# An attention loop that takes two steps per turn, in a fused two-layer graph network

## Chip, cores and metric

The kernel runs on one core of one Trainium2 chip. The metric is the device time of one execution in microseconds; runs of a kernel are taken beside runs of the kernel before on the same chip. All runs told here are of the same (fast) state: a kernel's executions agree within 0.25%.

## The reference, cut to what matters

Layer 0 (a graph convolution with batch norm) ends with `out = batchnorm(h @ W2.T)`; its last normalization is left to the second layer's loop. The changed loop computes layer 1 for 16 batches of 1024 nodes with 256 features, all in float32:

```python
x  = layernorm(x + layer0(x))                        # x1 in the kernel
c  = mean over features of x                         # cs, crow
A  = |(|sigmoid(c[m] - c[n]) - 0.5|) - 0.5| * 2      # per batch, 1024 x 1024
Wg = adj * A                                         # wg
q  = relu((x^T @ Wg) * para)                         # pg -> qT, 4 heads of 64
k, v = split(x @ kv_w)                               # pk -> kT, pv -> v
out = softmax(q k^T * scale) v                       # s -> e -> o, denominators pd
x  = layernorm(x + out)                              # pf, r
```

## The kernel before

Names that the profile uses: `s` scores (TensorE), `e` their exponentials (ScalarE), `acc` sums of e (VectorE), `o` values. One **step** handles two heads, 512 queries and 256 keys; 16 steps make a batch, which I call a **window**. Beside the attention of batch b, a schedule `at` prepares batches b+1 (keys, values, graph matmuls) and b+2 (load, batch norm, layer norm, transposes, graph weights).

```python
        ps_s = pool("ps_s", 2, space=PSUM)   # scores: 2 tiles of two banks
        ps_o = pool("ps_o", 1, space=PSUM)
        ps_t = pool("ps_t", 3, space=PSUM)   # shared by py, px, pc, pk, pv, pg, pd, pf
        # ... (cut)
        def bn2(b, j):                       # VectorE: batch norm of layer 0 (yt)
            for c in range(CT):
                t = yts[b, j][:, c, :]
                nc.vector.tensor_scalar(t, t, s2[:, c : c + 1], t2[:, c : c + 1], op0=OP.mult, op1=OP.add)
        # ...
        def ln1_a(b, j):                     # TensorE py, then VectorE
            p = ps_t.tile([P, FB], F32, tag="t", name="py")
            for c in range(CT):
                nc.tensor.transpose(p[:, ts(c, P)], yts[b, j][:, c, :], ident)
            # ... x1 = p + x, statistics
        def x1_t(b, j):                      # TensorE px, then ScalarE
            p = ps_t.tile([P, FB], F32, tag="t", name="px")
            for c in range(CT):
                nc.tensor.transpose(p[:, ts(c, P)], x1s[b, j][:, ts(c, P)], ident)
            nc.scalar.copy(x1Ts[b][:, :, ts(j, P)], p[:, :C].rearrange("p (c n) -> p c n", c=CT))
        # ...
        def wg_b(b, i):                      # VectorE, behind two ScalarE passes of wg_a
            t = wgs[b, i]
            nc.vector.scalar_tensor_tensor(t, t, 1.0, adj_sb[:, i, :], op0=OP.add, op1=OP.mult)
        # ... (cut: crow (pc), keys (pk), values (pv), graph (pg), scores (s), attend (o),
        #      dens (pd), finish_a (pf), finish_b)
        def put(w, s, f, *a):
            at.setdefault(w * NS + s, []).append((f, a))

        for b in range(B):
            put(b - 2, 4, begin, b)
            for j in range(NT):
                put(b - 2, 3 + j, load, b, j)
                put(b - 2, 4 + j, bn2, b, j)
                put(b - 2, 5 + j, ln1_a, b, j)
                put(b - 2, 6 + j, ln1_b, b, j)
                put(b - 2, 7 + j, x1_t, b, j)
            put(b - 2, 7 + NT, crow, b)
            for i in range(NT):
                put(b - 2, 8 + NT + i, wg_a, b, i)
                put(b - 2, 8 + NT + i, wg_b, b, i)
            # ... (cut: keys, values, graph of b - 1; dens and finish of b)

        for g in range(min(at), max(last, nsteps - 1) + 1):
            if 0 <= g + 1 < nsteps:
                scores(g + 1)
                exps(g + 1)
            if 0 <= g < nsteps:
                sums(g)
            for f, a in at.get(g, []):
                f(*a)
            if g == load_weights_at:
                load_weights()
            if 0 <= g < nsteps:
                attend(g)
```

Of the kernel before, what the change touches and what calls it, by code (L numbers as in the profile page):

```python
# [22 lines left out]
def gnn_norm_attention_kernel(  # L23
# [276 lines left out]
    def load_weights():  # L300
        nc.sync.dma_start(kvw, kv_w.rearrange("(c p) f -> p c f", p=P))
        for i in range(0, NT, 2):
            nc.sync.dma_start(
                adj_sb[:, i : i + 2, :], adj[i * P : (i + 2) * P, :].rearrange("(c p) m -> p c m", p=P)
            )
        nc.sync.dma_start(para_sb, para.rearrange("o (c p) h w -> p c (o h w)", p=P))
# [14 lines left out]
    def fast():  # L321
      with ExitStack() as fx:
        pool = lambda name, bufs, **k: fx.enter_context(tc.tile_pool(name=name, bufs=bufs, **k))
        ldp = pool("ldp", 3)
        x1p = pool("x1p", 21)
        x1Tp = pool("x1Tp", 1)
        crp = pool("crp", 1)
        wgp = pool("wgp", NT)
        kp = pool("kp", 2 * CT)
        qp = pool("qp", CT + 1)  # L330
        vp = pool("vp", 2)
        ep = pool("ep", 5)
        accp = pool("accp", 3)
        otp = pool("otp", 3)
        sm = pool("sm", 4)
        rp = pool("rp", 4)
        ps_s = pool("ps_s", 2, space=PSUM)
        ps_o = pool("ps_o", 1, space=PSUM)
        ps_t = pool("ps_t", 3, space=PSUM)
# [104 lines left out]
        def step(g):  # L444
            b, s = divmod(g, NS)
            hf, pair, cp = s // (NP * NT // 2), s // (NT // 2) % NP, s % (NT // 2)
            return b, hf, pair, cp

        def scores(g):
            b, hf, pair, cp = step(g)  # L450
            for a in range(2):
                cb = 2 * cp + a
                t = ps_s.tile([P, 2, FB], F32, tag="s", name=f"s{g}_{a}")
                for h in range(2):
                    nc.tensor.matmul(  # L455
                        t[:, h, :],
                        kTs[b, pair][h * HD : (h + 1) * HD, ts(cb, P)],
                        qTs[b, pair][h * HD : (h + 1) * HD, ts(hf, FB)],
                        start=True,
                        stop=True,  # L460
                    )
                S[g, a] = t

        def exps(g):
            for a in range(2):
                E[g, a] = ep.tile([P, 2, FB], F32, tag="e", name=f"e{g}_{a}")
                nc.scalar.activation(E[g, a], S.pop((g, a)), AF.Exp)  # L467

        def sums(g):
            b, hf, pair, cp = step(g)  # L470
            if cp == 0:
                ACC[b, hf, pair] = accp.tile([P, 2, FB], F32, tag="acc", name=f"acc{g}")
                nc.vector.tensor_add(ACC[b, hf, pair], E[g, 0], E[g, 1])
            else:
                for a in range(2):
                    nc.vector.tensor_add(ACC[b, hf, pair], ACC[b, hf, pair], E[g, a])  # L476

        def attend(g):
            b, hf, pair, cp = step(g)
            if cp == 0:  # L480
                O[b, hf, pair] = ps_o.tile([P, FB], F32, tag="o", name=f"o{g}")
            for a in range(2):
                cb = 2 * cp + a
                for h in range(2):
                    nc.tensor.matmul(  # L485
                        O[b, hf, pair][h * HD : (h + 1) * HD, :],
                        vs[b][:, cb, pair * P + h * HD : pair * P + (h + 1) * HD],
                        E[g, a][:, h, :],
                        start=(cb == 0),
                        stop=(cb == NT - 1),  # L490
                    )
                E.pop((g, a))
            if cp == NT // 2 - 1:
                t = otp.tile([P, FB], F32, tag=f"ot{pair}", bufs=2 - pair, name=f"ot{g}")
                nc.scalar.copy(t, O.pop((b, hf, pair)))
                OT[b, hf, pair] = t
# [38 lines left out]
        at = {}  # L535
# [32 lines left out]
                put(b, s + 1 + i % (FB // P), finish_a, b, i)  # L568
                put(b, s + 2 + i % (FB // P), finish_b, b, i)

        last = max(at)
        nsteps = B * NS
        load_weights_at = -2 * NS + 3
        for g in range(min(at), max(last, nsteps - 1) + 1):
            if 0 <= g + 1 < nsteps:
                scores(g + 1)
                exps(g + 1)
            if 0 <= g < nsteps:
                sums(g)
            for f, a in at.get(g, []):  # L580
                f(*a)
            if g == load_weights_at:
                load_weights()
            if 0 <= g < nsteps:
                attend(g)

    fast()


# [169 lines left out]
```

## Time and profile before

| | kernel before |
|---|---|
| time, median of four runs | 2861.15 us (2859.72 to 2862.74) |
| span of the profiled run | 2855.9 us |
| one window, 16 steps | 115.08 us |
| idle of TensorE in a window | 1.32 us, before the pc transposes |

The window is the distance between the starts of the first s burst of one batch and of the next. Only windows 0 to 13 prepare a batch two ahead; window 14 prepares only one ahead, window 15 none. The prediction below shows the lines that carry the reading: TensorE is the bound, so look for time between matmul starts and for its waits.

### The profile page before, as it was taken

The numbers are of one execution on the slowest core, as the hardware profiler recorded it, in microseconds if no ns is written. First come the engines' busy times: TensorE is split into PE (matmuls) and PEld (weight loads), VectorE is DVE, ScalarE is ACT, GpSimd is POOL, SyncE is SP. The second block draws the span as 40 slices with busy tenths as digits, with TensorE's granted clock in tenths as the row PEclk, the third lists the DMA queues.
The fourth block names the chain that finished last, engine by engine and source line by source line (L and its number), as shares of the span: only waits on it lengthen the run. The fifth ranks groups of instructions, "written<-read, shape, count | busy, mean of one in ns | idle before, by whom it ended". The sixth has DMA issues, their size and how long they took to land.

```text
span 2855.9 us, 25725 instructions
## 1 busy us (share of the span) xinstructions
PE 2751.3 (96%) x9426; PEld 1170.7 (41%) x9426; DVE 1502.2 (53%) x2717; ACT 1162.0 (41%) x1487; POOL 377.5 (13%) x523
## 2 busy tenths in 40 slices
PE   7999999999899599999999999999999999999997
PEld 5444444444344244434434344344343443434332
DVE  3011111012444457667686686776766857668556
ACT  1111111112741155645546455364464553644633
POOL 0000000000000112122121221221212212113012
PEclk7999999999999699999999999999999999999998
DMA  3121122120463410001010010010100100101000
GB/s 104 59 88 59 74 88 78 70 103 0 158 232 111 151 30 25 28 19 39 19 32 30 16 43 24 23 35 18 38 30 15 41 20 29 34 13 43 8 10 22
DMA packets 109988, 146.97 MB, mean 51 GB/s; under 512 B 10272, under 2 KB 92704, under 8 KB 103712
## 3 DMA queue, kind: packets, MB, share of 16 engines
q1 hardware_dynamic: 109856, 145.27, 14.9%
q8 instruction: 76, 1.25, 0.2%
q14 instruction: 56, 0.46, 0.1%
HBM read 86.52 MB, written 58.72 MB: 51 GB/s over the span
## 4 chain that ended last, share of the span: by engine, by line
PE 96%; DVE 2%; DMA 1%; POOL 0%; ACT 0%; issue 0%; SPq 0%; POOLq 0%; ACTq 0%
PE s L455 17%; PE o L485 17%; PE pg L435 16%; PE pa L201 15%; PE po L264 8%; PE ph L214 8%; PE pk L408 4%; PE pv L419 4%; PE pf L515 2%; PE pd L504 1%; PE py L364 1%; PE px L377 1%; PE pd L172 1%; PE pc L388 1%; PE pf L516 0%; DMA yt<-yT 0%
## 5 line engine op out<-in xcount | busy, mean ns | idle before, releaser
L467 ACT ACTIVATE e<-s 128x1024 f32<-128x1024 f32 x512 | 496.5, 1022 | 480.7 <-PE s L455 479.4
L455 PE MATMUL s<-qT,kT 64*128 64x512 f32 x2048 | 508.7, 615 | 0.0
L485 PE MATMUL o<-e,v 128*64 128x512 f32 x2048 | 495.7, 605 | 0.0
L476 DVE TENSOR_TENSOR acc<-acc,e 128x1024 f32<-128x1024 f32 x384 | 468.7, 1221 | 41.7 <-ACT e L467 27.8
L435 PE MATMUL pg<-wg,x 128*128 128x512 f32 x1024 | 477.2, 604 | 0.2 <-ACT x1T L378 0.2
L201 PE MATMUL pa<-AhT,x 128*128 128x512 f32 x1024 | 441.9, 592 | 0.0
L233 DVE BATCH_NORM_STATS2 st<-ph 128x6 f32<-128x512 f32 x128 | 89.4, 699 | 570.4 <-ACT hT L232 570.4
L455 PEld LDWEIGHTS s<-qT,kT 64*128 64x128 f32 x2048 | 176.2, 186 | 327.0 <-issue 286.8
L201 PEld LDWEIGHTS pa<-AhT,x 128*128 128x128 f32 x1024 | 194.5, 190 | 244.4 <-issue 244.2
L435 PEld LDWEIGHTS pg<-wg,x 128*128 128x128 f32 x1024 | 182.2, 190 | 240.3 <-issue 219.8
L400 DVE SCALAR_TENSOR_TENSOR wg<-wg,adj_sb 128x1024 f32<-128x1024 f32 x128 | 156.8, 1225 | 227.2 <-ACT wg L396 227.2
L214 PE MATMUL ph<-agg,W1T 128*128 128x512 f32 x512 | 222.2, 592 | 0.0
L485 PEld LDWEIGHTS o<-e,v 128*64 128x64 f32 x2048 | 124.3, 136 | 225.4 <-issue 212.5
L208 ACT COPY agg<-pa 128x512 f32<-128x512 f32 x64 | 37.5, 586 | 402.3 <-PE pa L201 402.3
L68 POOL TENSOR_TENSOR rs_a<-rs_a,mhalf 128x1 f32<-128x1 f32 x128 | 195.9, 1530 | 10.6
L378 ACT COPY x1T<-px 128x256 f32<-128x256 f32 x128 | 47.4, 370 | 357.5 <-PE px L377 357.5
L66 POOL TENSOR_SCALAR rs_z<-mv_z 128x1 f32<-128x1 f32 x128 | 40.8, 319 | 1000.2 <-DVE mv_z L313 1000.2
L264 PE MATMUL po<-hL,W2T 128*128 128x512 f32 x384 | 165.0, 592 | 0.0
L214 PEld LDWEIGHTS ph<-agg,W1T 128*128 128x128 f32 x512 | 97.3, 190 | 122.5 <-issue 122.5
L395 ACT ACTIVATE wg<-crow,cs 128x1024 f32<-128x1024 f32 x128 | 147.0, 1149 | 0.0
L396 ACT ACTIVATE wg<-wg 128x1024 f32<-128x1024 f32 x128 | 135.3, 1057 | 4.1
L232 ACT COPY hT<-ph 128x512 f32<-128x512 f32 x128 | 75.0, 586 | 144.7 <-PE ph L214 144.7
(97 smaller groups left out, 2229.5 us busy)
## 6 DMA issues: line engine op xcount, KB each, us to landing
h<-hT SPq DMA_DIRECT2D x24, 1024.0 KB, 3.8
hL<-h SPq DMA_DIRECT2D x24, 1024.0 KB, 6.2
x<-in_x_dram SPq DMA_DIRECT2D x16, 1024.0 KB, 5.5
yT<-y SPq DMA_DIRECT2D x32, 512.0 KB, 3.6
yt<-yT SPq DMA_DIRECT2D x128, 128.0 KB, 2.6
xr<-in_x_dram SPq DMA_DIRECT2D x128, 128.0 KB, 2.3
out_dram<-r SPq DMA_DIRECT2D x128, 128.0 KB, 1.7
A<-in_adj_dram SPq DMA_DIRECT2D x4, 1024.0 KB, 8.1
```

Of the source, the lines that this page charges most:

```text
L68: nc.gpsimd.tensor_tensor(dst, src, mhalf[:, :n], OP.pow)
L201: nc.tensor.matmul(p, xts[b][:, k, ts(c, P)], AhT[:, k, ts(h, FB)], start=(k == 0), stop=(k == NT - 1),)
L214: nc.tensor.matmul(p, W1T[:, k, ts(f, P)], aggT[b][:, k, ts(h, FB)], start=(k == 0), stop=(k == CT - 1),)
L264: nc.tensor.matmul(p, W2T[:, k, ts(c, P)], hT[u][:, k, :], start=(k == 0), stop=(k == HT - 1))
L395: nc.scalar.activation(t, crows[b], AF.Abs, bias=css[b][:, i : i + 1], scale=-1.0)
L396: nc.scalar.activation(t, t, AF.Tanh, scale=-0.5)
L400: nc.vector.scalar_tensor_tensor(t, t, 1.0, adj_sb[:, i, :], op0=OP.add, op1=OP.mult)
L435: nc.tensor.matmul(pg[b], x1s[b, k][:, ts(c, P)], wgs[b, k][:, ts(h, FB)], start=(k == 0), stop=(k == NT - 1))
L455: nc.tensor.matmul(t[:, h, :], kTs[b, pair][h * HD : (h + 1) * HD, ts(cb, P)], qTs[b, pair][h * HD : (h + 1) * HD, ts(hf, FB)], start=True ...
L467: nc.scalar.activation(E[g, a], S.pop((g, a)), AF.Exp)
L476: nc.vector.tensor_add(ACC[b, hf, pair], ACC[b, hf, pair], E[g, a])
L485: nc.tensor.matmul(O[b, hf, pair][h * HD : (h + 1) * HD, :], vs[b][:, cb, pair * P + h * HD : pair * P + (h + 1) * HD], E[g, a][:, h, :], ...
```

## The change

The intent: between scores (64 rows of the array), the other stages (full array) and values (64 columns) TensorE pays for each change of block (0.15 to 0.20 us, worked out in the prediction below). Two steps per turn make one block of the other stages and one burst of values out of two, so two of the six blocks of two steps go (16 in a window).

```diff
-        ldp = pool("ldp", 3)
-        x1p = pool("x1p", 21)
+        ldp = pool("ldp", 2)
+        x1p = pool("x1p", 20)
...
-        ep = pool("ep", 5)
+        ep = pool("ep", 6)
...
-        rp = pool("rp", 4)
+        rp = pool("rp", 3)
...
-        for g in range(min(at), max(last, nsteps - 1) + 1):
-            if 0 <= g + 1 < nsteps:
-                scores(g + 1)
-                exps(g + 1)
-            if 0 <= g < nsteps:
-                sums(g)
-            for f, a in at.get(g, []):
-                f(*a)
-            if g == load_weights_at:
-                load_weights()
-            if 0 <= g < nsteps:
-                attend(g)
+        for g in range(min(at) // 2 * 2, max(max(at), nsteps - 1) + 1, 2):
+            both = [k for k in (g, g + 1) if 0 <= k < nsteps]
+            if 0 <= g + 2 < nsteps:
+                scores(g + 2)
+                exps(g + 2)
+            for k in (g, g + 1):
+                if k in both:
+                    sums(k)
+                for f, a in at.get(k, []):
+                    f(*a)
+                if k == load_weights_at:
+                    load_weights()
+            if 0 <= g + 3 < nsteps:
+                scores(g + 3)
+                exps(g + 3)
+            for k in both:
+                attend(k)
```

## The prediction

> **What bounds the kernel now.** I read the page's summary and chain first, then the timeline of TensorE and of all engines in the attention loop, then the start times of single matmuls.
>
> ```profile
> PE 2751.3 (96%) x9426; PEld 1170.7 (41%) x9426; DVE 1502.2 (53%) x2717; ACT 1162.0 (41%) x1487; POOL 377.5 (13%) x523
> ...
> PE 96%; DVE 2%; DMA 1%; POOL 0%; ACT 0%; issue 0%; SPq 0%; POOLq 0%; ACTq 0%
> ```
>
> TensorE is busy 96% of the span, and the chain that ended last runs through it for 96%. So only two things count: time between one matmul's start and the next that does no work, and waits of TensorE.
>
> ```profile
> 1508.80 1.99 PE L455 MATMUL s<-qT,kT 64*128 64x512 f32 x8
> 1510.72 1.06 PE L504 MATMUL pd<-acc,ones 128*32 128x512 f32 x8
> 1511.71 3.70 PE L408 MATMUL pk<-x1T,kvw 128*128 128x512 f32 x8
> 1515.34 1.94 PE L485 MATMUL o<-e,v 128*64 128x512 f32 x8
> 1517.21 1.99 PE L455 MATMUL s<-qT,kT 64*128 64x512 f32 x8
> ```
>
> This is one step: scores s (64 rows of the array, two matmuls side by side), the other stages X (mostly the full array), values o (64 columns, side by side). Inside a block, matmul starts are 0.429 us apart (s and o: per side-by-side pair). So four pairs should take 1.72 us, yet s takes 1510.72-1508.80 = 1.92 and o 1517.21-1515.34 = 1.87; the eight pk should take 3.43 and take 3.63. **Each change of block costs**: about 0.20 us for s, 0.15 for o, 0.20 for X that begins with a 512-wide matmul, and 0.15 for X that begins with transposes (pf or py; from the single starts: 0.057 at the second, 0.094 at the exit). The single starts show the same figures in every step.
>
> TensorE waits little in the loop: 1.32 us once in 16 steps, before the pc transposes. A window (16 steps, one batch) is 115.08 us throughout (s bursts at 1499.83 and, 16 steps later, 1614.91).
>
> **What the Trainium skill says.** "TensorEngine Tiling (Array Packing)", Key Properties: changing the tiling mode, not just the tile, drains TensorE. The trace agrees, with 0.15 to 0.20 us a block. "TensorE: Matmul & The Clock Gate", Part 1: an idle window of about 3.4 us halves the clock. The trace shows one case near the loop: after 3.17 us idle the clock was 0.50 for 3.4 us, while the 1.32 us gaps never did it:
>
> ```profile
> 1011.74 0.54 PE L364 MATMUL py<-ident,yt 128*128 128x128 f32 x2 [3.17 <-ACT wg L395]
> 1012.16 5.37 PE L435 MATMUL pg<-wg,x 128*128 128x512 f32 x8
> ```
>
> (Eight pg take 3.4 us at full clock, so this cost nearly 2 us.) "Perfetto Trace Analysis", Identifying the Most-Contended Engine: the same gap repeating on the engine that should be saturated can mean too little PSUM for the next tile. That bears on the rotating PSUM buffers below: four banks of scores, one of values, three shared by all X tiles. The kernel before shows no such gap.
>
> **The change, part by part.** Two steps become one turn: s, X of both, s, o, o. Arithmetic and instruction counts stay the same.
>
> (1) *Fewer block changes.* Two steps had 2 s + 2 o + X + X' blocks; a turn has two s blocks, but one o block and one X block. Saved per turn: 0.145 (o) plus 0.198 or 0.151 (X'). In a window, the odd steps 1, 3, 5, 9, 11 begin with transposes and 7, 13, 15 with 512-wide matmuls: 5 x 0.296 + 3 x 0.343 = 2.5 us. Over 16 windows: **-40 us**.
>
> (2) *New waits.* The exponentials of step g+2 start 1.18 us after their scores and take 1.94, so the second s burst finds its PSUM free as soon as X lasts 0.3 us; X is 4 us and more. The buffers for exponentials (six) free in the order of the o matmuls, 3.6 us long, before the next turn's scores need them. So **the burst itself costs no wait**. But X of the odd step now follows X of the even step directly, with no o and s (about 3.8 us) between, and its inputs come from the even step. I went through all eight turns with the order and the waits of the built program and durations of the trace. Turns (0,1), (2,3), (12,13) show none, (14,15) only the old 1.3 us. The others:
>
> *Turn (4,5).* The transposes py of the next batch's first tile need its batch norm, which on VectorE stands behind the graph weight wg of step 4, which waits for ScalarE's two wg passes, which stand behind the exponentials. The timeline before shows this chain:
>
> ```profile
> 1538.62 1.99 PE L455 MATMUL s<-qT,kT 64*128 64x512 f32 x8
> ...
> 1541.62 1.15 ACT L395 ACTIVATE wg<-crow,cs 128x1024 f32<-128x1024 f32 x1
> ...
> 1542.81 1.06 ACT L396 ACTIVATE wg<-wg 128x1024 f32<-128x1024 f32 x1
> ...
> 1543.89 1.23 DVE L400 SCALAR_TENSOR_TENSOR wg<-wg,adj_sb 128x1024 f32<-128x1024 f32 x1 [0.99 <-ACT wg L396]
> ...
> 1545.04 0.60 DVE L355 TENSOR_SCALAR yt<-yt,s,t 128x128 f32<-128x128 f32 x2
> ...
> 1546.54 0.44 PE L364 MATMUL py<-ident,yt 128*128 128x128 f32 x2
> ```
>
> The norm ends 1545.64-1538.62 = 7.0 us after the scores. Before, py came 7.9 us after them: hidden. In the turn, TensorE has only s (1.92), pf (0.39) and pv (1.73) before py, so it is there at 4.04 and waits to about 7.0: **2.9 us**.
>
> *Turns (8,9) and (10,11).* All X tiles share three PSUM buffers, and the pg group holds one. In the changed program pf waits for ScalarE's copy of px, and the second py waits for the copy of the second px, issued just before it. The loop through ScalarE is known from this:
>
> ```profile
> 1561.00 0.38 PE L377 MATMUL px<-ident,x 128*128 128x128 f32 x2
> 1561.22 0.38 PE L364 MATMUL py<-ident,yt 128*128 128x128 f32 x2
> ...
> 1561.55 0.35 ACT L378 COPY x1T<-px 128x256 f32<-128x256 f32 x1
> ```
>
> From the second px (1561.11) to the end of its copy, plus 0.05 to the next start, is 0.85 us. pf would start 0.33 after that px and py 0.11: waits of 0.52 and 0.73, **1.25 us a turn**. *Turn (6,7)*: py waits about 0.25 for a batch norm.
>
> Per window 2.9 + 2 x 1.25 + 0.25 = 5.65 us, against 2.5 saved: a window of about 118.2. Only windows 0 to 13 prepare a batch two ahead, so this comes 14 times: **+79 us**.
>
> (3) *Buffers.* One load buffer fewer: in the lead-in before, the fourth load already waited for the second tile's transposes, as with two buffers, so about 0. x1 and r: their users are on one engine in order or have a step of slack: 0.
>
> (4) *Clock.* The 2.9 us gap is near the 3.17 that halved the clock. Each hit costs about 1.7 us (half of 3.4); I take a third of 14: **+8 us**.
>
> Sum: 2860 - 40 + 79 + 8 = **2907 us**.
>
> **Rivals.** *A: only the saving counts*, the other engines run ahead of my walk: 2820. For it: VectorE and ScalarE are only 53% and 41% busy. Against: the 7.0 us chain is measured from the scores that start it, and the queues are in order, so average slack does not shorten it. *B: the clock falls in every window*: +24 rather than +8, so 2923. For: a gap not much longer did it once. Against: the window must lie almost exactly over a shorter gap. *C: the second s burst waits for ScalarE* in many turns, 0.5 us in 128 turns: 2970. For: ScalarE also carries 2.2 us of wg a step in half the loop. Against: the exponentials stand before wg in its queue, so they are done at 3.1 us, and X lasts longer.
>
> **Range and chances.** Without clock loss 2899, with all of it 2923; my waits may be wrong by a quarter (20 us), mostly downwards if one of the small ones is hidden. Range 2884 to 2927. Slower by over 2% means over 2917: 0.25. Faster by over 2% means under 2803, which even rival A misses: 0.02. Within 2%: 0.73.
>
> **What would show it.** Blocks: the second o burst following the first with 0.43 us between starts, and o to s once a turn. Waits: a gap of about 2.9 us before py once a window, ended by the batch norm; gaps near 0.5 before pf and 0.7 before py, twice each, ended by ScalarE's x1T copy; a window of 118.2 us and no wait before s. Clock: some stretches at 0.50 after the long gap. Wrong if py's gap is under 1 us, if s waits, or if a window is under 116 us.

## The result, and the profile after

The changed kernel took 2924.53 us (median of four runs, 2922.24 to 2925.47), against 2861.15 for the kernel before. The ratio is 1.022, with an interval of 1.0202 to 1.0238: slower by just over 2%. A ratio here is the mean time of one kernel's fast runs over that of the other's of the same rounds, so it isn't quite the ratio of the medians quoted.

The page's summary and chain of the changed kernel:

```profile
PE 2758.5 (94%) x9426; PEld 1196.4 (41%) x9426; DVE 1494.8 (51%) x2717; ACT 1163.0 (40%) x1487; POOL 410.6 (14%) x523
...
PE 91%; DVE 3%; ACT 3%; issue 1%; DMA 1%; POOL 1%; SPq 0%; DVEq 0%; POOLq 0%; ACTq 0%
```

The instruction counts are those of before. TensorE fell from 96% to 91% of the chain, and VectorE and ScalarE took 3% each. This already says that the end now waits for them in places. The timeline of TensorE in the turn (4,5) of one window (start, us, then engine, line and operation; the brackets give the idle time before and what ended it) shows the largest:

```profile
1443.26 1.99 PE L455 MATMUL s<-qT,kT 64*128 64x512 f32 x8
...
1445.56 1.89 PE L419 MATMUL pv<-kvw,x1T 128*128 128x256 f32 x8
1450.07 0.73 PE L364 MATMUL py<-ident,yt 128*128 128x128 f32 x2 [2.62 <-DVE yt L355]
1450.73 3.31 PE L455 MATMUL s<-qT,kT 64*128 64x512 f32 x8
```

The last line is a second loss: eight s matmuls take 3.31 us instead of 1.99. The same stretch on ScalarE and VectorE tells why py is late:

```profile
1446.26 1.15 ACT L395 ACTIVATE wg<-crow,cs 128x1024 f32<-128x1024 f32 x1
...
1447.44 1.06 ACT L396 ACTIVATE wg<-wg 128x1024 f32<-128x1024 f32 x1
...
1448.53 1.23 DVE L400 SCALAR_TENSOR_TENSOR wg<-wg,adj_sb 128x1024 f32<-128x1024 f32 x1 [0.99 <-ACT wg L396]
...
1449.67 0.60 DVE L355 TENSOR_SCALAR yt<-yt,s,t 128x128 f32<-128x128 f32 x2
```

The batch norm (L355) stands behind L400, which waits for ScalarE's L396. VectorE itself was idle for 0.99 us with the norm's inputs long there (their load was issued at 1439.52 and landed 2.5 us later): a queue in order, not a lack of speed.

Cut into stretches of the clock monitor (the clock in the trace changes only on a grid of 3.41 us), the same place reads so (busy us of each engine with its instructions, then PEclk, the granted clock, then DMA):

```profile
core 0: us, PE busy (x) PEld busy (x) DVE busy (x) ACT busy (x) POOL busy (x), PEclk, DMA share, GB/s
1446.61:1450.03 3.42, 0.84 (x4) 0.39 (x3) 2.36 (x6) 3.38 (x4) 0.79 (x2) 1.00 0.03 10
1450.03:1453.44 3.41, 3.37 (x8) 1.55 (x10) 3.38 (x5) 1.06 (x1) 0.00 (x0) 0.50 0.00 0
```

After a stretch with 0.84 us of TensorE work, the next ran at half clock. **This happens in every one of the 14 windows.** The small waits of a pair of steps further on, in turn (8,9) and again in (10,11), are the predicted ones (TensorE's timeline again):

```profile
1477.74 0.38 PE L377 MATMUL px<-ident,x 128*128 128x128 f32 x2
1477.96 0.38 PE L364 MATMUL py<-ident,yt 128*128 128x128 f32 x2
1478.59 0.44 PE L515 MATMUL pf<-ident,ot 128*128 128x128 f32 x2 [0.24 <-ACT x1T L378]
...
1481.55 0.38 PE L377 MATMUL px<-ident,x 128*128 128x128 f32 x2
1482.39 0.44 PE L364 MATMUL py<-ident,yt 128*128 128x128 f32 x2 [0.46 <-ACT x1T L378]
```

(Idle is counted from the modelled end of the matmul before. From start to start, pf comes 0.41 us late and py 0.63; the start after each is late by another 0.05, so they cost 0.46 and 0.68, together 1.14 us a turn.) The reading that the prediction took from "Perfetto Trace Analysis" (section Optimization Strategy: a gap that repeats on the engine that should be busy can mean too few PSUM buffers) fits: the gaps of 0.24 and 0.46 us come twice in each window, each behind the copy that frees a shared buffer.

The fewer blocks are there too. At the end of that turn (4,5) the sixteen o take 3.59 us from their first start to the next s, where two bursts took 2 x 1.87 before, and the other stages of both steps of turn (6,7) stand in one block, from 1459.48 to 1466.65:

```profile
1453.97 3.65 PE L485 MATMUL o<-e,v 128*64 128x512 f32 x16
1457.56 1.99 PE L455 MATMUL s<-qT,kT 64*128 64x512 f32 x8
...
1466.65 1.99 PE L455 MATMUL s<-qT,kT 64*128 64x512 f32 x8
```

Other readings from starts in the trace:

| us | before | after |
|---|---|---|
| windows 1 to 13 | 115.08 | 119.77, 119.69, then falling to 119.47 |
| windows 0 to 13 together | 1607.2 | 1668.5 |
| window 14 | 111.43 | 109.25 |
| stretches at half clock, windows 0 to 13 | 0 | 14 |

Window 14, without the preparation of a batch two ahead and so without the new waits, is 2.2 us *faster*: the saving is real.

### The profile page after: what moved, and what is told of

Read it like the earlier page. It is cut to its first block, busy times and chain, and to the rows that moved or that the text cites. A ratio compares the mean times of both kernels' runs of the same rounds, so it can differ in the third digit from the quotient of the medians.

```text
span 2922.3 us, 25725 instructions
## 1 busy us (share of the span) xinstructions
PE 2758.5 (94%) x9426; PEld 1196.4 (41%) x9426; DVE 1494.8 (51%) x2717; ACT 1163.0 (40%) x1487; POOL 410.6 (14%) x523
## 3 DMA queue, kind: packets, MB, share of 16 engines
q8 instruction: 76, 1.25, 0.2%
## 4 chain that ended last, share of the span: by engine, by line
PE 91%; DVE 3%; ACT 3%; issue 1%; DMA 1%; POOL 1%; SPq 0%; DVEq 0%; POOLq 0%; ACTq 0%
PE s L455 17%; PE pg L435 15%; PE o L485 15%; PE pa L201 15%; PE po L264 8%; PE ph L214 8%; PE pk L408 4%; PE pv L419 3%; PE py L364 1%; PE pf L515 1%; PE pd L504 1%; PE px L377 1%; PE pd L172 1%; ACT x1T L378 1%; ACT e L467 1%
## 5 line engine op out<-in xcount | busy, mean ns | idle before, releaser
L455 PE MATMUL s<-qT,kT 64*128 64x512 f32 x2048 | 527.1, 634 | 0.5 <-ACT e L467 0.5
L485 PE MATMUL o<-e,v 128*64 128x512 f32 x2048 | 467.5, 598 | 0.0
L400 DVE SCALAR_TENSOR_TENSOR wg<-wg,adj_sb 128x1024 f32<-128x1024 f32 x128 | 155.7, 1216 | 290.6 <-ACT wg L396 290.6
L455 PEld LDWEIGHTS s<-qT,kT 64*128 64x128 f32 x2048 | 182.8, 193 | 268.8 <-issue 157.5
L485 PEld LDWEIGHTS o<-e,v 128*64 128x64 f32 x2048 | 135.8, 136 | 319.9 <-issue 319.9
L66 POOL TENSOR_SCALAR rs_z<-mv_z 128x1 f32<-128x1 f32 x128 | 65.4, 511 | 978.5 <-DVE mv_z L313 978.5
L364 PE MATMUL py<-ident,yt 128*128 128x128 f32 x256 | 60.1, 314 | 81.5 <-DVE yt L355 62.9
L396 ACT ACTIVATE wg<-wg 128x1024 f32<-128x1024 f32 x128 | 135.3, 1057 | 4.1
```

Of the source, the lines that this page charges most:

```text
L396: nc.scalar.activation(t, t, AF.Tanh, scale=-0.5)
L455: nc.tensor.matmul(t[:, h, :], kTs[b, pair][h * HD : (h + 1) * HD, ts(cb, P)], qTs[b, pair][h * HD : (h + 1) * HD, ts(hf, FB)], start=True ...
L485: nc.tensor.matmul(O[b, hf, pair][h * HD : (h + 1) * HD, :], vs[b][:, cb, pair * P + h * HD : pair * P + (h + 1) * HD], E[g, a][:, h, :], ...
```

## Experiments

My theory: the saving is about 2.5 us a window, and it is overpaid by the wait for the batch norm (2.9), the waits for ScalarE's x1T copies (2 x 1.1) and the clock, which the long gap halves (some 1.4). Rivals: the buffer counts cost; paired blocks save nothing; the small waits are hidden; the clock costs nothing of its own.

**1. e1_norm_first**, the changed kernel with the batch norm emitted first in each step:

```diff
-                for f, a in at.get(k, []):
+                todo = at.get(k, [])
+                for f, a in [t for t in todo if t[0] is bn2] + [t for t in todo if t[0] is not bn2]:
```

> The changed kernel, but in each step the batch norm of the next tile (bn2) is issued on VectorE ahead of the step's other stages instead of behind the graph weight wg. My theory (the 2.6 us gap of TensorE before py in turn (4,5) is the queue behind wg, and this gap alone lowers the clock): the gap and the clock drops go; a window falls from 119.47 to about 114.9 us (2.9 wait, 1.5 clock, 0.2 in turn (6,7)), the time from 2924 to about 2860. Rival (the clock drops for another reason, such as the longer bursts of half-array matmuls): the gap goes but the clock still shows 0.50 once a window, about 2881.

Measured: 2861.91 us, ratio to the kernel before 1.0003 (0.9986 to 1.0020); window 114.83. TensorE's timeline of the turn (4,5), in which py follows pv without a wait:

```profile
1432.91 1.89 PE L419 MATMUL pv<-kvw,x1T 128*128 128x256 f32 x8
1434.64 0.38 PE L364 MATMUL py<-ident,yt 128*128 128x128 f32 x2
```

No stretch at half clock is left in the windows. So one emission order costs the whole loss of 63 us, through wait and clock together. The window also measures the saving: with the small waits of 2 x 1.14 still there, the blocks must have given 115.08 + 2.28 - 114.83 = 2.53 us (predicted 2.5).

**2. e2_px_early**, the transposes of x1 (px) moved right behind the step's first graph matmul, so that ScalarE's copy has time:

```diff
-                for f, a in at.get(k, []):
+                todo = [t for t in at.get(k, []) if t[0] is not x1_t]
+                n = 1 + next((n for n, t in enumerate(todo) if t[0] is graph), -1)
+                for f, a in todo[:n] + [t for t in at.get(k, []) if t[0] is x1_t] + todo[n:]:
```

> The changed kernel, but the px transposes of a step stand behind its first graph matmul instead of behind its last, so that a graph matmul lies between px and the next tile that takes its PSUM buffer. My theory (pf and the second py wait for ScalarE's copy of px, because they reuse its buffer): the four gaps (0.24 and 0.46 of idle, 0.41 and 0.63 between starts) go, about 0.4 may come back before px in turn (6,7); a window without clock loss falls by 1.8 to 116.2, 26 us in all. The long gap stays. Clock: if the drops are locked to the window's length (119.47 us is 35 times 3.413), that lock is broken at this length and fewer than 14 windows show a drop, so 2880 to 2895; if each long gap always costs a drop, 14 drops and about 2899.

Measured: 2905.73 us, ratio 1.0150 (1.0133 to 1.0167). A window without a clock drop is 117.09, one with a drop 118.74: **a drop costs 1.65 us**, seen here within one run. Drops came in 9 of 14 windows. A window without a drop was to be 116.2, and with fewer than 14 drops the time 2880 to 2895: the gain of the move was half of what I expected. The waits for ScalarE went, but new ones came. In turn (6,7) x is not normalized yet when px comes so early; in turn (10,11) pg waits 0.24 us for VectorE's qT, and px then for VectorE's L366, which reads py out of a shared buffer:

```profile
1460.74 0.44 PE L377 MATMUL px<-ident,x 128*128 128x128 f32 x2 [0.18 <-DVE x L319]
...
1491.13 0.44 PE L377 MATMUL px<-ident,x 128*128 128x128 f32 x2 [0.44 <-DVE x L366]
```

The two scores that span turn (8,9) came 1.14 us closer (9.47 for 10.61), those of turn (10,11) not at all (10.78 for 10.76): there the new waits cost what the old ones did.

**3. e3_both**, the two edits together:

```diff
-                for f, a in at.get(k, []):
+                todo = [t for t in at.get(k, []) if t[0] is bn2]
+                todo += [t for t in at.get(k, []) if t[0] not in (bn2, x1_t)]
+                n = 1 + next((n for n, t in enumerate(todo) if t[0] is graph), -1)
+                for f, a in todo[:n] + [t for t in at.get(k, []) if t[0] is x1_t] + todo[n:]:
```

> Both edits in one: no wait but the old one before pc and about 0.4 in turn (6,7), no clock drop. My theory: only the saving from fewer changes of block is left, a window of about 113.0 (115.08 before, less 2.5, plus 0.4), and a time of about 2834, some 1% under the kernel before. Rival (the longer turn itself costs, or the saving from fewer block changes is not real): a window of 115 or more, no faster than before.

Measured: 2849.32 us, ratio 0.9957 (0.9941 to 0.9974); window 114.11, no clock drop. The direction held, the size (113.0 and 2834 were expected) fell short by the same new waits.

**4. e4_warm**, which leaves the wait for the batch norm and fills it: the pv matmuls ahead of the gap are done twice.

```diff
-            for a in range(2):
+            for a in (0, 1, 0, 1) if j == NT - 2 else (0, 1):
```

> The changed kernel with useless work added: the pv matmuls just ahead of the long gap are done twice (1.73 us more of TensorE per window; the result is the same). My theory (the clock drops because TensorE is inactive for nearly a whole monitor window): the gap shrinks to about 0.9 us, py still waits for the same batch norm at the same time, no clock drop, so a window of about 118.0 and a time of about 2904: faster by 20 us with 28 us more work. Rival (the clock loss is not due to this gap): no change, 2924, or slower if the added work delays anything.

Measured: 2906.26 us, ratio 1.0152 (1.0135 to 1.0169), window 118.11 throughout, clock 1.00 in all windows. The timeline of TensorE:

```profile
1441.37 3.62 PE L419 MATMUL pv<-kvw,x1T 128*128 128x256 f32 x16
1445.88 0.59 PE L364 MATMUL py<-ident,yt 128*128 128x128 f32 x2 [0.89 <-DVE yt L355]
```

py still starts when VectorE lets it, but 1.73 us of useless work stand in the gap, and the kernel is **18 us faster**. So the clock has a cost of its own: windows 0 to 13 took 1648.4 us here and 1668.5 in the changed kernel, a difference of 20.1 us or 1.43 a drop. Against e1 (114.83) the window 118.11 gives the cost of VectorE's lateness alone: 3.28 us (2.98 in turn (4,5), 0.31 in turn (6,7); predicted 2.9 and 0.25).

**5. bufs_only**, the kernel before with the changed buffer counts alone:

```diff
-        ldp = pool("ldp", 3)
-        x1p = pool("x1p", 21)
+        ldp = pool("ldp", 2)
+        x1p = pool("x1p", 20)
...
-        ep = pool("ep", 5)
+        ep = pool("ep", 6)
...
-        rp = pool("rp", 4)
+        rp = pool("rp", 3)
```

> The kernel before with the buffer counts of the changed one alone (weights of the load 2 for 3, 20 for x1, 6 for e, 3 for the rest). My theory: no effect, window 115.08 us, time 2861 +-4, same order of work. Rival: the buffers carry a part of the loss, then the time is 2870 or more.

Measured: 2861.33 us, ratio 0.9999 (0.9982 to 1.0016), window 115.08. The buffers carry nothing in the loop of single steps. No run has the paired loop with the old counts; but px_crow below has the changed counts and waits only 0.24 us in a window, for VectorE.

**6. off_lock2.** Why did *every* window of the changed kernel lose clock, though a gap of 2.6 us is shorter than a stretch of 3.41 and could fall across two? The windows converge on 119.47 us, which is 35 x 3.413. Theory: the loop locks onto the monitor's grid. If the whole drop hits work, the window is 119.77 and the next gap comes 0.3 us later on the grid; then a part of the slow stretch falls into the gap itself, where it costs nothing, and the window shrinks, until it is a whole number of stretches. The test lengthens the loop elsewhere, in turn (2,3):

```diff
-            for a in range(2):
+            for a in (0, 1, 0) if j == 0 else (0, 1):
```

> The changed kernel with one values matmul of one tile done once more in turn (2,3), well away from the long gap: 0.86 us more TensorE work per window, so a window without a clock drop is 118.11 + 0.86 = 118.97 us. Theory of the lock: with the 119.47 us period left, the gap falls at varying places against the monitor's 3.41 us windows, drops come in 4 to 9 of the 14 windows, and the time is about 2920 to 2926, no longer than the changed kernel in spite of 12 us more work. Rival, each long gap costs a drop wherever it falls: 14 drops, time 2936 or more.

Measured: 2931.22 us (2930.70 to 2932.64), ratio 1.0247 (1.0230 to 1.0264). Drops came in 9 of 14 windows, at a gap of 2.61 us (2.90 in the first) in all 14: a window without one takes 118.97, as worked out. Three stretches from the windows view, each beginning with the monitor's stretch that holds the gap (columns as above):

```profile
1206.79:1210.20 3.41, 0.80 (x5) 0.28 (x3) 2.39 (x6) 3.35 (x5) 0.79 (x2) 1.00 0.00 0
1210.20:1213.61 3.41, 3.41 (x9) 1.19 (x8) 3.38 (x4) 0.53 (x1) 0.00 (x0) 0.50 0.03 12
...
1326.25:1329.67 3.42, 1.46 (x7) 0.95 (x5) 2.33 (x5) 3.39 (x5) 0.79 (x2) 1.00 0.02 4
1329.67:1333.08 3.41, 2.75 (x12) 1.17 (x14) 3.38 (x6) 1.66 (x2) 0.00 (x0) 1.00 0.00 0
...
1684.65:1688.07 3.42, 1.36 (x7) 0.86 (x5) 2.33 (x5) 3.39 (x5) 0.79 (x2) 1.00 0.00 0
1688.07:1691.48 3.41, 2.85 (x8) 1.53 (x10) 3.38 (x7) 1.56 (x2) 0.00 (x0) 0.50 0.00 0
1691.48:1694.90 3.42, 3.42 (x10) 0.68 (x10) 3.35 (x8) 0.00 (x0) 1.04 (x2) 0.50 0.39 114
```

The first is wholly inside: 0.80 us busy, a drop. The second falls across a border, 1.46 and 2.75 busy: no drop. The third, 1.36 busy, drops, its next stretch still holds 0.56 us of the gap, and the clock stays low for a second one. So the rival (each long gap costs a drop wherever it falls) is refuted by five windows, and the place on the grid decides. But my number for the time missed too: I had not known the double drops, which came 3 times. The nine drops hold 12 slow stretches and cost 17.8 us, 1.48 for each. The lock that I describe fits the changed kernel's convergence to 119.47 and the lost drops here, as well as those of e2_px_early, another period. The changed kernel's trace shows its beginning and its end: the part of the gap that lies in the slow stretch grows from 0 to 0.27 us while the window shrinks from 119.77 to 119.47. Why 0.27 us of it gives back 0.30 is argued, not shown.

**7. px_last**, batch norm first and px just ahead of the step's *last* graph matmul (late enough for VectorE, early enough for ScalarE):

```diff
-                for f, a in at.get(k, []):
+                todo = [t for t in at.get(k, []) if t[0] is bn2]
+                todo += [t for t in at.get(k, []) if t[0] not in (bn2, x1_t)]
+                n = max((n for n, t in enumerate(todo) if t[0] is graph), default=0)
+                for f, a in todo[:n] + [t for t in at.get(k, []) if t[0] in (x1_t,)] + todo[n:]:
```

> The changed kernel with the batch norm first in each step and the transposes of x1 just ahead of the step's last graph matmul: the gaps before pf and py should go without the new ones of the early placement. Theory: window 112.7 us, time about 2830, gaps left only the old 1.33 before pc and some 0.1 before pg. Rival: the waits come back elsewhere as in the early placement, window 114 and 2849.

Measured: 2834.02 us, ratio 0.9909 (0.9892 to 0.9925), window 113.05. Both small waits are gone; a wait of 0.24 before pg in turn (10,11) came, which costs 0.50 from start to start and is why the window missed 112.7. Against e1 this gives the small waits again: 114.83 - 113.05 + 0.50 = 2.28, twice 1.14.

**8. px_crow**, where the crow transposes (pc) move too:

```diff
-                for f, a in at.get(k, []):
+                todo = [t for t in at.get(k, []) if t[0] is bn2]
+                todo += [t for t in at.get(k, []) if t[0] not in (bn2, x1_t, crow)]
+                n = max((n for n, t in enumerate(todo) if t[0] is graph), default=0)
+                for f, a in todo[:n] + [t for t in at.get(k, []) if t[0] in (x1_t, crow)] + todo[n:]:
```

> As the one before, and the crow transposes too ahead of the last graph matmul, so that pc need not wait behind qT on VectorE: the old gap of 1.33 us should go. Theory: window 111.4 us, time about 2810. Rival: pc's wait only moves to another consumer, time as the one before.

Measured: 2812.18 us, ratio 0.9831 (0.9815 to 0.9848), window 111.51. TensorE's timeline of px_last around pc, with the old wait:

```profile
1495.06 3.60 PE L435 MATMUL pg<-wg,x 128*128 128x512 f32 x8
1499.98 1.09 PE L388 MATMUL pc<-ident,cs 128*128 128x128 f32 x8 [1.33 <-DVE cs L382]
```

and of px_crow, without it, with the last graph matmuls behind:

```profile
1491.41 1.04 PE L388 MATMUL pc<-ident,cs 128*128 128x128 f32 x8
1492.28 1.02 PE L435 MATMUL pg<-wg,x 128*128 128x512 f32 x2
```

**9. before_order**, the kernel before with px_crow's reordering inside each step, to see what the pairing itself is worth. The edit is that of px_crow, in the loop of single steps:

```diff
-            for f, a in at.get(g, []):
+            todo = [t for t in at.get(g, []) if t[0] is bn2]
+            todo += [t for t in at.get(g, []) if t[0] not in (bn2, x1_t, crow)]
+            n = max((n for n, t in enumerate(todo) if t[0] is graph), default=0)
+            for f, a in todo[:n] + [t for t in at.get(g, []) if t[0] in (x1_t, crow)] + todo[n:]:
```

> The kernel before, one step per turn, with only the reordering inside a step that px_crow has (batch norm first; transposes of x1 and of the crow ahead of the step's last graph matmul). It tells how much of px_crow's 49 us belongs to the reordering alone. Theory: the reordering removes only the old wait of 1.33 us (some 1.45 start to start) per window before pc, so the window is 113.6 us and the time about 2840, and the two-step turn is worth the remaining 28 us or so. Rival: the reordering does it all, 2815.

Measured: 2842.47 us (2836.47 to 2842.90), ratio 0.9936 (0.9919 to 0.9953), window 113.56. So of px_crow's 49 us about 19 belong to the order alone, and the two-step turn, once its large waits are gone, gives 30 us: 113.56 - 111.51 = 2.05 us a window. The wait of 0.24 is still in it and costs 0.50; without it the blocks give 2.55, which agrees with the 2.53 of e1.

**10. single_tail**, the changed kernel with single steps in the last batch (the loop advances by 1 from `nsteps - NS`, and skips scores that the last pair has already issued):

```diff
-        for g in range(min(at) // 2 * 2, max(max(at), nsteps - 1) + 1, 2):
+        single = nsteps - NS
+        g, end = min(at) // 2 * 2, max(max(at), nsteps - 1) + 1
+        while g < end:
+            w = 1 if g >= single else 2
...
+            g += w
```

> The changed kernel with single steps for the last batch (16 steps), where no next batch is prepared. Theory: there the pairing costs, because the denominators and the finishing of the last tiles wait for VectorE, so single steps give back about 3 to 5 us: last window near 65.4 us (15 intervals) for 66.2, time about 2920. Rival: the pairing saves its 2.4 us there as predicted and the miss is elsewhere, then the time is 2927. The interval of three rounds is about as wide as the difference, so the profile's last window decides.

Measured: 2922.68 us (2922.39 to 2922.82), not told apart from the changed kernel by time. The trace resolves it: from the first s of window 15 to the end of the last pf, the changed kernel takes 80.76 us, this one 79.00. (My figure of 65.4 for 15 intervals compared the wrong things: the first single step still carries the turn before, so the intervals sum to 69.66.) In its last window the changed kernel has four waits of TensorE that single_tail has not: 0.34 us twice before pf, 0.27 before s and, the largest, 1.14 before pd. Its timeline there:

```profile
2897.41 1.05 PE L504 MATMUL pd<-acc,ones 128*32 128x512 f32 x4
2899.61 1.05 PE L504 MATMUL pd<-acc,ones 128*32 128x512 f32 x4 [1.14 <-DVE acc L476]
```

and in single_tail the eight pd run through:

```profile
2897.73 1.48 PE L504 MATMUL pd<-acc,ones 128*32 128x512 f32 x8
```

**11. best_tail**, px_crow with single steps in the last batch, so the edits of 8 and 10 together:

> px_crow with single steps for the last batch. Theory: as in single_tail, 3 to 5 us below px_crow's 2812, so about 2808, with window 111.51. Rival: 2814.

Measured: 2809.45 us, ratio 0.9821 (0.9805 to 0.9838); the same part of the trace takes 78.98 us instead of 80.76, the same 1.8 us again. The gain is smaller than the 3 to 5 that I expected, and by time alone it is not told apart from px_crow. This is the fastest version here, 1.8% below the kernel before.

## Why the prediction was right or wrong

The range (2884 to 2927) held 2924.5, but near its upper end, and the class that I gave 0.73 (within 2%) was not the one that came; the ratio of 1.022 lies just beyond it. By the steps:

| step | predicted | measured | from |
|---|---|---|---|
| blocks, windows 0 to 14 | -2.51 each, -38 | -2.53 each, -38 | e1; window 14 alone -2.18 |
| wait for batch norm, turns (4,5) and (6,7) | 2.9 + 0.25 | 2.98 + 0.31 | e4 less e1 |
| waits for the x1T copies | 2 x 1.25 | 2 x 1.14 | starts; e1 less px_last |
| the three waits, 14 windows | +79 | +78 | 14 x 5.57 |
| buffers | 0 | 0 | bufs_only |
| clock | +8 | +20 | after less e4 |
| last window | -2.4 | +1.8 | single_tail |
| sum | +47 | +62 | measured difference 63.4 |

**The mechanism was right**: small saving, larger waits, the engines and the lines that I named. The small waits came out 0.1 shorter each because the loop through ScalarE takes 0.74 us here; my 0.85 was read at a place where ScalarE was busy with L396 until about the copy's start. Rival A (only the saving counts) missed by 100 us; rival C (s waits for exponentials) doesn't show in the windows; s waits for them 0.27 us twice in the whole run, in its first window and its last.

**The term that was mis-sized is the clock.** I wrote "a third of 14", since the gap would have to lie almost exactly over a monitor stretch. Rival B, a drop in every window, is what happened. That its 2923 lies within 2 us of the measured time is partly luck: its 24 us for the clock was 4 too many, and the last window, 4 too few, made up for it. Two things were wrong in my step. The stretch need not be idle all through: idle times of 2.34 to 2.64 us in the 3.41 always sufficed in the changed kernel. And its place on the grid is not a free draw for each window: the period of the loop settled on 35 stretches, so that the gap met the same place each time. A drop costs 1.4 to 1.65, somewhat under my 1.7.

**The last window** is the smaller miss, 4 us. I counted its block saving without walking its turns; there no other stages give VectorE and ScalarE time, and the pairing makes pf, s and pd wait (2.1 us in the four waits of experiment 10).

## What to carry to other kernels

When two steps are merged, the order that hid a producer's latency is gone: walk the merged turn and put first, on each in-order engine, what the busiest engine needs next; here moving one small VectorE operation ahead of a waiting one was worth 63 us, and with two more moves the order turned a loss of 2.2% into a gain of 1.7%. A wait of TensorE that fills most of one stretch of the clock grid (2.6 of 3.4 us here) must be priced with the half-speed stretch behind it, and not in a small share of the turns: it came in 9 of 14 at two periods and in 14 of 14 where the loop had settled on the grid. Useless matmuls in such a gap are a quick test of it. And a transpose that shares its buffers had a best place here that is neither first nor last: too early it waited for its producer, too late the next tile waited for its copy.

## What the Trainium skill lacked or had wrong

- "TensorE: Matmul & The Clock Gate" (Part 1, and the table of "Why this matters for your kernels"): it speaks of at least one idle window of about 3.4 us, and of no gaps over about 3 us. Its free-running window agrees with the grid of 3.413 us here, but less idle time suffices: from 1.76 us of one window on (e2_px_early), from 2.04 on (off_lock2) and at 2.34 to 2.64 (the changed kernel) the clock was halved for the next, while up to 1.57 in e2_px_early and 1.96 in off_lock2 it wasn't (idle counted to the modelled ends of matmuls). The limit differs a little between the two kernels, and I can't say by what; the stretches with the least idle that dropped began in the gap in e2_px_early (py and s behind it), and with pv in off_lock2 (the gap behind it).
- The same page: it doesn't say how busy a slow window must be for the clock to come back. Here, with 0.50 to 0.58 us idle in the slow window the clock stayed at 0.50 (the three double drops in off_lock2); with up to 0.27 it came back (the changed kernel).
- No page says that a loop can lock onto that window: the changed kernel's period went to 119.47 us, 35 windows of 3.413, and lost clock in 14 of 14 turns; off_lock2, with the same gap at another period, in 9 of 14.
- "TensorEngine Tiling (Array Packing)", Key Properties: it says that a change of mode drains TensorE, but not for how long. Here each block of another shape cost 0.15 to 0.20 us, and removing 16 of them from a window gave 2.53 us (e1_norm_first).
